# A gated graph network with graph attention on one core: the row of scores through DRAM, pieces made in other ticks, and a new prologue

## The chip, the cores and the metric

The kernel runs on one core of a Trainium2 chip. The metric is device time in microseconds (us) of one launch; the kernel before takes 2248.21 us (median of three runs, 2247.11 to 2249.96). Five engines run side by side, each through its own list of instructions in order: TensorE (PE in the profile, with PEld for its weight loads), VectorE (DVE), ScalarE (ACT), GpSimd (POOL) and SyncE (SP), which here only issues DMA transfers. TensorE multiplies and transposes; its results land in PSUM[...].

## The reference, cut to what matters

There are 64 graphs of 256 nodes with 256 features. Layer 0 is three rounds of a gated graph network with a residual and a layer norm, layer 1 is graph attention with the same.

```python
def _L0_gnn_ref(x, adj, weight, w_ih, w_hh, b_ih, b_hh):
    A = (adj != 0).astype(x.dtype)
    h = x
    for i in range(3):
        m = jnp.einsum('bnd,de->bne', h, weight[i])
        aggr = jnp.einsum('bst,bsd->btd', A, m)
        h = _gru_cell(aggr, h, w_ih, w_hh, b_ih, b_hh)   # r, z, n: sigmoid, sigmoid, tanh
    return h

def _L1_gnn_ref(h, adj, W, a):
    Wh = jnp.matmul(h, W)
    s1 = jnp.einsum('bnf,f->bn', Wh, a[:Fout, 0])
    s2 = jnp.einsum('bnf,f->bn', Wh, a[Fout:, 0])
    e = jax.nn.leaky_relu(s1[:, :, None] + s2[:, None, :], negative_slope=ALPHA)
    attn = jax.nn.softmax(jnp.where(adj > 0, e, NEG_INF), axis=2)
    return jnp.matmul(attn, Wh)

x = _layernorm(x + _L0_gnn_ref(x, adj, ...), axis=-1)
return _layernorm(x + _L1_gnn_ref(x, adj, ...), axis=-1)
```

For each node `n` the attention needs `s2` of every other node side by side in one row, whereas the projection leaves `s2` as a column, one node to a partition. How that column becomes a row is one of the things that change.

## The kernel before

The kernel works on pairs of graphs; there are 32. To keep nearly full precision[...], each operand is cut into pieces: `H` (upper), `L` (lower, source minus `H`) and `D` (a scaled cross term). A gate product is then three matmuls for each 128 x 512 block, two into bank `a` and one into bank `b`, joined by ScalarE and VectorE.

**Ticks.** The program order is made by a small clock. TensorE's gate matmuls are written out in groups of six, and after each group the clock moves by one tick; everything else (aggregation, transposes, attention) is a step that is hung on a tick and is written into its engine's list when the clock reaches it. A block (one round of one pair) has 12 ticks. In the steady state three pairs are under way, so a **turn** has three blocks (rounds 0, 1 and 2 of three pairs) and 36 ticks, and the attention of a fourth pair, with its 72 ticks, lies over two turns.

```python
def product(dst, o, parts, bias=None):
    a, b = bank("pga"), bank("pgb")
    todo = [(a, w[k], m[k], d) for w, m in parts for k in (0, 1) for d in range(C)]     # H, L
    ends = len(todo) - 1
    todo += [(b, w[2], m[2], d) for w, m in parts for d in range(C)]                    # D
    step = len(todo) // len(parts)
    for n, (pt, w, m, d) in enumerate(todo):
        nc.tensor.matmul(pt, w[:, d, o * P:(o + 1) * P], m[:, d, :], ...)               # L369
        if (n + 1) % step == 0 and n + 1 < len(todo):
            tick()
    nc.scalar.activation(dst, a, ..., scale=1.0 + U)                                     # L374, L376
    tick()
    nc.vector.scalar_tensor_tensor(dst, b, -1.0 / U, dst, op0=ALU.mult, op1=ALU.add)    # L378
# ... r, n, z, t for each half e of the features; then tanh, blend (POOL L395, L396), h (DVE L408)
```

A block's input is prepared one block ahead by `front`. `pace` gives the ticks: `turn` (transpose), `split` (`hi`), `rest` (`lo`), `aggregate` (A times hi and lo), `a_upper`, `a_rest`, then the pieces of `h`.

```python
def turn(d):
    s = pairs[p]
    if i == 0:
        src[d] = nodes(s.x, d)
        to_T(s.x, s.hT, d)                                    # L269
    else:
        src[d] = from_T(s.hT, d).rearrange(...)               # L275
def split(d):
    nc.scalar.copy(hi[d], src[d])                             # L306
def rest(d):
    lower(nc.gpsimd if i == 0 else nc.vector, lo[d], src[d], hi[d])      # L132
# ... h_upper (ACT L129), h_lower (POOL L132), h_cross (DVE L135), aggregate (PE L340)
for d in range(C):
    for dt, step in zip(pace[0], (turn, split, rest, aggregate, a_upper, a_rest)):
        at(t + dt + d, lambda step=step, d=d: step(d))
for dt, step in zip(pace[1], (h_upper, h_lower, h_cross)):
    at(t + dt, step)
LOOSE = (2, 3, 4, 6, 7, 8), (5, 8, 10)
```

The attention of a pair, with `t` the tick at which its last block ended (cut; `again`, `halves`, `back`, `join` fetch x and turn the sum back to rows of nodes):

```python
def project(k):
    nc.tensor.matmul(pts[k][:, :D + 2], s.vT[:, d, k * P:(k + 1) * P], gw[:, d, :], ...)  # L493
def spread(k):
    rs = s.rs[:, k:k + 1]
    for dst, src in ((s.s1[:, k:k + 1], pts[k][:, D:D + 1]),
                     (s.s2[:, k, :], pts[k][:, D + 1:D + 2].to_broadcast([P, P])),
                     (s.wh[:, k // C, k % C, :], pts[k][:, :D])): ...     # ACT L502, DVE L504
def rows():
    pts[0] = bank("s2")
    for k in range(K):
        nc.tensor.transpose(pts[0][:, k * P:(k + 1) * P], s.s2[:, k, :], ident)           # L512
def scores():                                                                             # L516
    nc.scalar.activation(s.sc[:, k, :], pts[0][...], AF.Prelu, bias=s.s1[:, k:k + 1], alpha=ALPHA)
def masked():
    nc.vector.copy_predicated(flat(s.sc), flat(s.mask), neg.to_broadcast([P, K * N]))     # L525
# reduce (max, L527), exps (L530), weights_T (L540), combine (L548), add (L554), layer norm, store
```

In the main loop, `begin` (L283, the ones of `adj`) is hung on tick 1 of the front of a new pair, the loads of the next `x` on 7, `masking` (L289) on 19 and the next `adj` on 20. Ahead of the loop a prologue loads and cuts the weights.

Of the kernel before, what the change touches and what calls it, by code (L numbers as in the profile page):

```python
# [26 lines left out]
def kernel(  # L27
# [89 lines left out]
    def flat(t):  # L117
        return t.rearrange("p a b -> p (a b)")
# [63 lines left out]

    wh_n = load_rows(w_hh, ("hH", "hL"), nc.sync)
    wi_n = load_rows(w_ih, ("aH", "aL"), nc.scalar)
# [7 lines left out]
    load_x(0)  # L192
    load_adj(0)
    make_identity(nc, ident)
    nc.gpsimd.memset(half, -0.5)
    nc.gpsimd.memset(neg, NEG_INF)
# [11 lines left out]
    def rows_T(src, use):  # L208
        for c in range(C):
            for o0, o1, t in src:  # L210
                pt = bank("pw")
                for o in range(o1 - o0):
                    nc.tensor.transpose(pt[:, o * P:(o + 1) * P], t[:, o, c * P:(c + 1) * P], ident)
                use(c, o0 * P, o1 * P, pt[:, :(o1 - o0) * P])

    def square_T(src, name):
        pt = bank("pw")
        for e in range(C):
            for d in range(C):
                nc.tensor.transpose(pt[:, (e * C + d) * P:(e * C + d + 1) * P],  # L220
                                    src[:, d, e * P:(e + 1) * P], ident)
        dst = work.tile([P, K, P], F32, tag="hi1", name=name, bufs=1)
        nc.scalar.copy(flat(dst), pt)
        return dst.rearrange("p k n -> p (k n)").rearrange("p (e d) -> p e d", e=C)

    def fold(i, wT, d):
        for o0, o1 in ((0, 512), (512, O)):
            pt = bank("pw")
            for e in range(C):
                nc.tensor.matmul(pt[:, :o1 - o0], wT[:, e, d * P:(d + 1) * P], wih(e, o0, o1),  # L230
                                 start=(e == 0), stop=(e == C - 1))
            cut_weight([t[:, d, o0:o1] for t in wc[i]], pt[:, :o1 - o0], f"{i}_{d}_{o0}")
# [45 lines left out]
    def begin(p):  # L278

        s = pairs[p] = Pair()  # L280
        s.x, s.adj = loaded.pop(p), loaded_adj.pop(p)
        s.A = work.tile([P, G, C, N], F32R, tag="A", name=f"A_{p}", bufs=3)
        nc.vector.tensor_scalar(s.A, s.adj, 0.0, None, op0=ALU.not_equal)  # L283
        s.hT = work.tile([P, C, GN], F32, tag="hT", name=f"hT_{p}", bufs=4)
# [6 lines left out]
    def front(p, i, t, pace):  # L291
# [4 lines left out]
        def turn(d):  # L296
            s = pairs[p]
            if i == 0:
                src[d] = nodes(s.x, d)
                to_T(s.x, s.hT, d)  # L300
            else:
                src[d] = from_T(s.hT, d).rearrange("p (k n) -> p k n", k=K)

        def split(d):
            hi[d] = work.tile([P, K, P], F32R, tag=f"hi{d}", name=f"hi{d}_{nm}", bufs=1)
            nc.scalar.copy(hi[d], src[d])  # L306

        def rest(d):
            lo[d] = work.tile([P, K, P], F32R, tag=f"lo{d}", name=f"lo{d}_{nm}", bufs=1)
            lower(nc.gpsimd if i == 0 else nc.vector, lo[d], src[d], hi[d])  # L310
# [5 lines left out]
        if i == 0:  # L316
            at(t + pace[0][1] + 2, stash)
# [124 lines left out]
    def attention(p, t):  # L442
# [7 lines left out]
        at(t + 5, again)  # L450
# [29 lines left out]
        for d in range(C):  # L480
            at(t + 22 + d, lambda d=d: halves(d))
            at(t + 23 + d, lambda d=d: back(d))
        for g in range(G):
            at(t + 29 + g, lambda g=g: join(g))
        at(t + 30, lambda: setattr(s, "rs", layer_norm(s.v, f"a_{p}", (t + 31, t + 33, t + 34, t + 49))))

        def project(k):
            if k == 0:
                s.s1 = work.tile([P, K], F32, tag="s1", name=f"s1_{p}")
                s.s2 = s.sc[:, :, :P]  # L490
            pts[k] = bank("pwh")
            for d in range(C):
                nc.tensor.matmul(pts[k][:, :D + 2], s.vT[:, d, k * P:(k + 1) * P], gw[:, d, :],  # L493
                                 start=(d == 0), stop=(d == C - 1))

        def spread(k):
            rs = s.rs[:, k:k + 1]
            for dst, src in ((s.s1[:, k:k + 1], pts[k][:, D:D + 1]),
                             (s.s2[:, k, :], pts[k][:, D + 1:D + 2].to_broadcast([P, P])),
                             (s.wh[:, k // C, k % C, :], pts[k][:, :D])):  # L500
                if k < 2:
                    nc.scalar.activation(dst, src, AF.Copy, scale=rs)  # L502
                else:
                    nc.vector.tensor_scalar(dst, src, rs, None, op0=ALU.mult)  # L504
        for k in range(K):
            at(t + 35 + k, lambda k=k: project(k))
            at(t + 36 + k, lambda k=k: spread(k))

        def rows():
            pts[0] = bank("s2")  # L510
            for k in range(K):
                nc.tensor.transpose(pts[0][:, k * P:(k + 1) * P], s.s2[:, k, :], ident)  # L512

        def scores():
            for k in range(K):
                nc.scalar.activation(s.sc[:, k, :], pts[0][:, (k // C) * N:(k // C + 1) * N], AF.Prelu,  # L516
                                     bias=s.s1[:, k:k + 1], alpha=ALPHA)
        at(t + 40, rows)
        at(t + 41, scores)

# [5 lines left out]
        at(t + 42, masked)  # L526
        at(t + 43, lambda: nc.vector.tensor_reduce(s.nm, s.sc, AX.X, ALU.max, negate=True))  # L527
# [4 lines left out]
        for k in range(K):  # L532
            at(t + 47 + k // 2, lambda k=k: exps(k))
        at(t + 52, lambda: nc.vector.reciprocal(s.sm, s.sm))
# [21 lines left out]
        for g in range(G):  # L556
            at(t + 53 + g, lambda g=g: weights_T(g))
            at(t + 54 + g, lambda g=g: nc.vector.tensor_copy(flat(s.sc[:, g * C:(g + 1) * C, :]), pts[g]))
            at(t + 57 + g, lambda g=g: combine(g))
            at(t + 58 + g, lambda g=g: add(g))  # L560
# [4 lines left out]
        at(t + 60, lambda: layer_norm(s.v, f"b_{p}", (t + 61, t + 64, t + 66, t + 70), store))  # L565
# [3 lines left out]
    LOOSE = (2, 3, 4, 6, 7, 8), (5, 8, 10)  # L569

# [4 lines left out]


    rows_T(wh_n, lambda c, o0, o1, pt: cut_weight([t[:, c, o0:o1] for t in whh], pt, f"h{c}_{o0}"))
    begin(0)
    masking(0)
    load_adj(1)  # L580
    rows_T(wi_n, lambda c, o0, o1, pt: evacuate(wih(c, o0, o1), pt))
    nc.vector.tensor_add(b_sum, bi, bh)
    wT = square_T(w_n[0], "wT_0")
    front(0, 0, clock[0], LOOSE)
    for d in range(C):
        fold(0, wT, d)
        tick(3)
# [13 lines left out]
    for n, (p, i) in enumerate(blocks):  # L601
        if n + 1 < len(blocks):
            np_, ni = blocks[n + 1]
            if ni == 0:
                after(1, lambda p=np_: begin(p))
            front(np_, ni, clock[0], CLOSE if n and np_ == blocks[n - 1][0] else LOOSE)
            if ni == 0:
                after(7, lambda p=np_: load_x(p + 1))
                after(19, lambda p=np_: masking(p))
                after(20, lambda p=np_: load_adj(p + 1))  # L610
# [35 lines left out]
```

## Time and profile before

| what | value |
|---|---|
| time, median of three | 2248.21 us |
| span of the profiled execution | 2247.1 us |
| TensorE busy | 2189.0 us (97%) |
| VectorE, ScalarE, GpSimd busy | 1728.2, 1556.4, 1535.2 us |
| one turn in the steady state | 67.4 us, 30 of them with all three blocks |
| mean granted TensorE clock | 0.990 |
| HBM traffic | 39 GB/s over the span |

A turn is the distance between equal instructions of two neighbouring pairs: the transposes of `back`, for example, are issued at 1011.75 us and again at 1079.20 us. The busy time of TensorE counts matmuls that overlap in its pipeline once, so a matmul's own duration (395 ns for one of 512 columns) is longer than its share of a full stream (234 ns, the distance of the starts). What a piece of TensorE work costs is therefore read from starts, not from durations.

### The profile page before, as it was taken

The numbers are of one execution on the slowest core, as the hardware profiler recorded it, in microseconds if no ns is written. First come the engines' busy times: TensorE is split into PE (matmuls) and PEld (weight loads), VectorE is DVE, ScalarE is ACT, GpSimd is POOL, SyncE is SP. The second block draws the span as 40 slices with busy tenths as digits, with TensorE's granted clock in tenths as the row PEclk, the third lists the DMA queues.
The fourth block names the chain that finished last, engine by engine and source line by source line (L and its number), as shares of the span: only waits on it lengthen the run. The fifth ranks groups of instructions, "written<-read, shape, count | busy, mean of one in ns | idle before, by whom it ended". The sixth has DMA issues, their size and how long they took to land.

```text
span 2247.1 us, 31126 instructions
## 1 busy us (share of the span) xinstructions
PE 2189.0 (97%) x10724; PEld 1813.6 (81%) x10724; DVE 1728.2 (77%) x2920; ACT 1556.4 (69%) x2899; POOL 1535.2 (68%) x1084
## 2 busy tenths in 40 slices
PE   7999999999999999999999999999999999999985
PEld 5788888888888888888888888888888888888864
DVE  4667778878778878778878778878778878778875
ACT  4566777677777677777677777677777677777665
POOL 5777667767667767667767667767667767667751
PEclk9999999999999999999999999999999999999997
DMA  3011111111111211112111111111111111111111
GB/s 113 29 38 38 34 42 57 57 48 38 42 43 57 57 47 38 41 45 57 57 48 38 41 45 57 57 48 38 40 46 57 57 48 38 39 47 38 29 38 47
DMA packets 130237, 105.30 MB, mean 47 GB/s; under 512 B 70368, under 2 KB 121824, under 8 KB 130080
## 3 DMA queue, kind: packets, MB, share of 16 engines
q1 hardware_dynamic: 128288, 101.47, 15.4%
q8 instruction: 86, 1.41, 0.3%
q10 hardware_dynamic: 1616, 1.57, 0.2%
q14 instruction: 71, 0.58, 0.1%
q0 software_dynamic: 176, 0.27, 0.1%
HBM read 52.96 MB, written 33.55 MB: 39 GB/s over the span
## 4 chain that ended last, share of the span: by engine, by line
PE 85%; POOL 10%; ACT 1%; DVE 1%; DMA 1%; issue 1%; POOLq 0%; SPq 0%; ACTq 0%; DVEq 0%
PE pga L369 42%; PE pgb L369 21%; PE pa L340 7%; PE po L548 5%; PE pwh L493 5%; POOL t L396 3%; PE pt L275 3%; POOL lo L132 2%; POOL t L395 2%; PE pt L540 1%; POOL n L405 1%; POOL n L401 1%; PE pt L269 1%; POOL rs_b L423 1%; DMA adj<-in_adj_dram 1%
## 5 line engine op out<-in xcount | busy, mean ns | idle before, releaser
L395 POOL TENSOR_TENSOR t<-hT,n 128x512 f32<-128x512 f32 x192 | 288.4, 1502 | 540.1 <-ACT n L387 540.0
L369 PE MATMUL pga<-hH,whhH_whh 128*128 128x512 f32 x1152 | 388.8, 418 | 0.0
L369 PE MATMUL pgb<-hD,whhD_whh 128*128 128x512 f32 x1152 | 362.0, 395 | 0.8 <-DVE hD L135 0.8
L369 PE MATMUL pga<-hL,whhL_whh 128*128 128x512 f32 x1152 | 362.3, 395 | 0.0
L405 POOL TENSOR_TENSOR n<-n,t 128x512 f32<-128x512 f32 x192 | 283.8, 1478 | 57.8 <-DVE t L378 45.5
L396 POOL TENSOR_TENSOR t<-t,z 128x512 f32<-128x512 f32 x192 | 280.6, 1461 | 15.1
L374 ACT ACTIVATE r<-pga 128x512 f32<-128x512 f32 x192 | 114.5, 596 | 235.6 <-PE pga L369 193.0
L369 PEld LDWEIGHTS pgb<-hD,whhD_whh 128*128 128x128 f32 x1152 | 216.3, 188 | 53.3 <-DVE hD L135 1.3
L369 PEld LDWEIGHTS pga<-hL,whhL_whh 128*128 128x128 f32 x1152 | 216.3, 188 | 51.6 <-POOL hL L132 0.2
L401 POOL TENSOR_TENSOR n<-n,r 128x512 f32<-128x512 f32 x192 | 252.8, 1317 | 0.8 <-DVE n L378 0.7
L132 POOL TENSOR_TENSOR hL<-hT,hH 128x1024 fp32r<-128x1024 f32 x96 | 243.8, 2540 | 8.9 <-ACT hH L129 8.9
L376 ACT ACTIVATE n<-pga,bh 128x512 f32<-128x512 f32 x192 | 131.6, 685 | 154.3 <-PE pga L369 154.0
L378 DVE SCALAR_TENSOR_TENSOR r<-pgb,r 128x512 f32<-128x512 f32 x192 | 131.7, 686 | 135.1 <-ACT r L374 75.2
L369 PEld LDWEIGHTS pga<-hH,whhH_whh 128*128 128x128 f32 x1152 | 196.0, 189 | 24.1
L340 PE MATMUL pa<-A,lo 128*128 128x256 f32 x768 | 195.9, 287 | 12.5 <-POOL lo L132 12.4
L340 PE MATMUL pa<-A,hi 128*128 128x256 f32 x768 | 196.5, 287 | 0.0
L378 DVE SCALAR_TENSOR_TENSOR n<-pgb,n 128x512 f32<-128x512 f32 x192 | 131.5, 685 | 67.5 <-ACT n L376 64.5
L387 ACT ACTIVATE z<-z,b_sum 128x512 f32<-128x512 f32 x192 | 141.6, 738 | 43.1 <-DVE z L378 42.7
L340 PEld LDWEIGHTS pa<-A,lo 128*128 128x128 f32 x768 | 146.9, 191 | 27.2 <-POOL lo L132 21.6
L378 DVE SCALAR_TENSOR_TENSOR t<-pgb,t 128x512 f32<-128x512 f32 x192 | 131.7, 686 | 38.5 <-ACT t L374 36.4
L135 DVE SCALAR_TENSOR_TENSOR hD<-hH,hT 128x1024 fp32r<-128x1024 f32 x96 | 156.5, 1630 | 0.0
L340 PEld LDWEIGHTS pa<-A,hi 128*128 128x128 f32 x768 | 146.8, 191 | 7.2
(136 smaller groups left out, 5495.6 us busy)
## 6 DMA issues: line engine op xcount, KB each, us to landing
x<-in_x_dram SPq DMA_DIRECT2D x32, 512.0 KB, 3.9
adj<-in_adj_dram SPq DMA_DIRECT2D x32, 512.0 KB, 3.9
xT<-hT SPq DMA_DIRECT2D x32, 512.0 KB, 2.6
vT<-xT SPq DMA_DIRECT2D x32, 512.0 KB, 3.3
out_dram<-v SPq DMA_DIRECT2D x32, 512.0 KB, 2.9
sc<-wh SPq DMA_TRANSPOSE x64, 3.1
w_n<-in_L_gnn_weight_dram ACTq DMA_DIRECT2D x3, 256.0 KB, 10.3
rows_aH<-in_L_gnn_w_ih_dram ACTq DMA_DIRECT2D x1, 512.0 KB, 6.1
```

Source lines behind the costliest of these rows:

```text
L132: eng.tensor_sub(dst, src, hi.bitcast(F32))
L135: nc.vector.scalar_tensor_tensor(dst, hi.bitcast(F32), 1.0 + U, src, op0=ALU.mult, op1=ALU.subtract)
L340: nc.tensor.matmul(pt[:, g * N:(g + 1) * N], h[:, g * C + c, :], s.A[:, g, c, :], start=(n == 0), stop=(n == len(todo) - 1))
L369: nc.tensor.matmul(pt, w[:, d, o * P:(o + 1) * P], m[:, d, :], start=n in (0, ends + 1), stop=n in (ends, len(todo) - 1))
L374: nc.scalar.activation(dst, a, AF.Copy, scale=1.0 + U)
L376: nc.scalar.activation(dst, a, AF.Identity, scale=1.0 + U, bias=bias)
L378: nc.vector.scalar_tensor_tensor(dst, b, -1.0 / U, dst, op0=ALU.mult, op1=ALU.add)
L387: nc.scalar.activation(dst, dst, func, bias=bias)
L395: nc.gpsimd.tensor_sub(t, h, n)
L396: nc.gpsimd.tensor_mul(t, t, z)
L401: after(2, lambda r=r, n=n: nc.gpsimd.tensor_mul(n, n, r))
L405: after(1, lambda n=n, t=t: nc.gpsimd.tensor_add(n, n, t))
```

## The change

It does five things.

1. **Row of s2 through DRAM.** `spread` writes `s1` and `s2` of a block as two neighbouring values. The column of `s2` is written to DRAM by one small DMA and read back by a second one, broadcast to all partitions. The four transposes, their bank and the two broadcast copies on ScalarE and two on VectorE go. ScalarE makes the scores from SBUF, in two steps.
2. **Pieces of x in other ticks.** For round 0 a third pace, FIRST, makes `hi` and `lo` of x two ticks earlier.
3. **Another timetable of the attention.** The layer norm, projection, combination and store come two to four ticks earlier; scores, masking and maximum come three ticks later than before.
4. **Mask and load of adj** move from ticks 19 and 20 to 22 and 23.
5. **Prologue in another order.** x is loaded and turned first, the ScalarE table for the sigmoid is loaded at once, the weights come in parts.

```diff
+    load_x(0)
     wh_n = load_rows(w_hh, ("hH", "hL"), nc.sync)
+    load_adj(0)
     wi_n = load_rows(w_ih, ("aH", "aL"), nc.scalar)
...
-    load_x(0)
-    load_adj(0)
...
+    nc.scalar.activation(warm, half, AF.Sigmoid)
...
         def rest(d):
-            lower(nc.gpsimd if i == 0 else nc.vector, lo[d], src[d], hi[d])
+            lower(nc.gpsimd if i == 0 and p else nc.vector, lo[d], src[d], hi[d])
...
-        at(t + 5, again)
+        at(t + 9, again)
...
-            at(t + 22 + d, lambda d=d: halves(d))
-            at(t + 23 + d, lambda d=d: back(d))
+            at(t + 21 + d, lambda d=d: halves(d))
+            at(t + 22 + d, lambda d=d: back(d))
         for g in range(G):
-            at(t + 29 + g, lambda g=g: join(g))
-        at(t + 30, lambda: setattr(s, "rs", layer_norm(s.v, f"a_{p}", (t + 31, t + 33, t + 34, t + 49))))
+            at(t + 26 + g, lambda g=g: join(g))
+        at(t + 27, lambda: setattr(s, "rs", layer_norm(s.v, f"a_{p}", (t + 28, t + 30, t + 31, t + 35))))
...
-            at(t + 35 + k, lambda k=k: project(k))
-            at(t + 36 + k, lambda k=k: spread(k))
+            at(t + 32 + k, lambda k=k: project(k))
+            at(t + 33 + k, lambda k=k: spread(k))

         def rows():
-            pts[0] = bank("s2")
-            for k in range(K):
-                nc.tensor.transpose(pts[0][:, k * P:(k + 1) * P], s.s2[:, k, :], ident)
+            s.row = far.tile([P, K], F32, tag="row", name=f"row_{p}", bufs=2)
+            nc.sync.dma_start(s.row, s.s12[:, 1, :])
+        def rows_back():
+            s.s2 = s.vT[:, 0, :]
+            nc.sync.dma_start(s.s2, s.row.rearrange("n k -> (n k)").partition_broadcast(P))
...
-        at(t + 40, rows)
-        at(t + 41, scores)
+        at(t + 37, rows)
+        at(t + 38, rows_back)
+        for g in range(G):
+            at(t + 43 + g, lambda g=g: scores(g))
...
-        at(t + 42, masked)
-        at(t + 43, lambda: nc.vector.tensor_reduce(s.nm, s.sc, AX.X, ALU.max, negate=True))
+        at(t + 45, masked)
+        at(t + 46, lambda: nc.vector.tensor_reduce(s.nm, s.sc, AX.X, ALU.max, negate=True))
...
-            at(t + 47 + k // 2, lambda k=k: exps(k))
-        at(t + 52, lambda: nc.vector.reciprocal(s.sm, s.sm))
+            at(t + 48 + k // 2, lambda k=k: exps(k))
+        at(t + 50, lambda: nc.vector.reciprocal(s.sm, s.sm))
...
-            at(t + 53 + g, lambda g=g: weights_T(g))
-            at(t + 57 + g, lambda g=g: combine(g))
+            at(t + 52 + g, lambda g=g: weights_T(g))
+            at(t + 55 + g, lambda g=g: combine(g))
...
+    FIRST = (2, 1, 2, 6, 7, 8), (5, 8, 10)
...
+    front(0, 0, clock[0] + 1, ((0, 1, 2, 9, 11, 12), (7, 8, 13)))
...
-                after(19, lambda p=np_: masking(p))
-                after(20, lambda p=np_: load_adj(p + 1))
+                after(22, lambda p=np_: masking(p))
+                after(23, lambda p=np_: load_adj(p + 1))
```

## The prediction

> **What bounds the kernel now.** I read the page's busy rows and chain first, then a table of stages (one turn of the steady state alone), then TensorE's waits in that stretch, and last the timelines of single engines, because in a kernel with a timetable only the order inside one turn tells what a moved step will meet.
>
> ```profile
> PE 2189.0 (97%) x10724; PEld 1813.6 (81%) x10724; DVE 1728.2 (77%) x2920; ACT 1556.4 (69%) x2899; POOL 1535.2 (68%) x1084
> PE 85%; POOL 10%; ACT 1%; DVE 1%; DMA 1%; issue 1%; POOLq 0%; SPq 0%; ACTq 0%; DVEq 0%
> ```
>
> TensorE is busy 97% of the span and carries 85% of the chain that ended last. The next view gives one turn (start:end and length, then busy time of PE, PEld, DVE, ACT, POOL, clock, DMA share, GB/s), and under it the whole list of TensorE's waits between 270 and 2090 us:
>
> ```profile
> 1012.00:1079.40 67.40, 67.10 (x333) 55.82 (x333) 53.24 (x91) 48.24 (x91) 47.37 (x33) 1.00 0.17 48
> PE pa L340 <- POOL lo L132: 8.1, 27, 0.3
> ```
>
> So in a turn of 67.40 us TensorE stands still for 0.30 us, always at the same place: the aggregation waits for `lo`, which GpSimd makes. The next busiest engine, VectorE, works 53.24 us of it. From the starts in TensorE's timeline the turn can be added up: 216 gate matmuls at 0.2335 us = 50.4; 48 of the aggregation at 0.119 = 5.7; 4 projections at 0.87 = 3.5; 2 combinations at 1.71 = 3.4; 9 groups of four transposes at 0.44 = 3.9; together 66.9, and about 0.56 for the wait. That gives 67.5, so nothing else is hidden in it. The kernel is bound by TensorE's own work. Only three things can move the time: TensorE work taken out, waits removed or created in the turn (each counts 30 times), and the two ends.
>
> [...] the spacing of the starts, not the 97%, is what I build on. [...] the 512 KB write of `xT` lands after 2.6 us, the read of `vT` after 3.3. No small DMA of this kind runs before the change[...]. [...] `hD`, the same instruction each time, takes 1.22 us or 2.32 us.
>
> **1. The transposes that go.** Their place in the turn:
>
> ```profile
> 1043.31 0.63 PE L369 MATMUL pga<-aH,wc0H_wc 128*128 128x512 f32 x2
> 1043.78 0.60 PE L512 MATMUL s<-ident,sc 128*128 128x128 f32 x4
> 1044.13 0.71 PE L369 MATMUL pga<-aL,wc0L_wc 128*128 128x512 f32 x2
> 1044.68 0.63 PE L369 MATMUL pgb<-hD,whhD_whh 128*128 128x512 f32 x2
> ```
>
> The four take 0.35 us to the next start, and the two matmuls behind them 0.55 instead of 0.47: 0.35 + 0.08, 0.44 us with rounding. Gain 0.44 us a turn. Two ScalarE copies of 364 ns and two VectorE copies of 342 ns also go; both engines are off the path.
>
> **2. The wait for lo.**
>
> ```profile
> 1025.31 0.28 PE L340 MATMUL pa<-A,hi 128*128 128x256 f32 x1
> 1025.89 0.39 PE L340 MATMUL pa<-A,lo 128*128 128x256 f32 x1 [0.30 <-POOL lo L132]
> 1026.11 0.28 PE L340 MATMUL pa<-A,hi 128*128 128x256 f32 x1
> ```
>
> From the first of these to the third there are 0.80 us; undisturbed it would be two steps of 0.12. The wait thus costs 0.56 us, of which only 0.30 is marked as idle. The cause is order: GpSimd makes this `lo` at 1024.54, behind the two steps of a blend (1021.66 and 1023.23). FIRST puts both `lo` at ticks 26 and 27, ahead of the blend at tick 29. GpSimd should then have the second some 2 us before TensorE wants it. Gain 0.56 us a turn.
>
> **3. The later masking.** Here I expect a loss. The page is no help; VectorE's list in ticks 6 to 10 is:
>
> ```profile
> 1046.97 1.40 DVE L525 COPY_PREDICATED_SCALAR sc<-mask,neg 128x1024 f32 x1 [0.40 <-ACT sc L516]
> 1049.01 1.21 DVE L527 TENSOR_REDUCE nm<-sc 128x4 f32<-128x1024 f32 x1
> 1050.14 0.95 DVE L289 TENSOR_SCALAR mask<-adj 128x1024 uint8<-128x1024 int32 x1
> 1052.20 0.68 DVE L378 SCALAR_TENSOR_TENSOR r<-pgb,r 128x512 f32<-128x512 f32 x1
> 1055.20 2.32 DVE L135 SCALAR_TENSOR_TENSOR hD<-hH,hT 128x1024 fp32r<-128x1024 f32 x1
> ```
>
> and TensorE's needs are (tick 8, and the first use of that `hD` in tick 13):
>
> ```profile
> 1051.69 0.63 PE L369 MATMUL pga<-hH,whhH_whh 128*128 128x512 f32 x2
> 1059.16 0.63 PE L369 MATMUL pgb<-hD,whhD_whh 128*128 128x512 f32 x2
> ```
>
> Now `hD` ends at 1057.52, 1.64 us before use. The three long VectorE steps lie in ticks 6 and 7, ahead of the result of `r`. After the change masking is at tick 9 (45), the maximum at 10 (46), `masking` at 10 (24 + 22 - 36), and all three enter the list ahead of `h_cross`, the step that makes `hD`, since they were hung up earlier. By starts they are 1.43 + 1.13 + 0.87 = 3.43 us. VectorE can't start them sooner, because `r` needs TensorE's tick 8. From tick 8 to the use TensorE has 7.47 us of work before and after. VectorE begins `r` 0.25 us sooner, with no backlog, so `hD` comes 3.2 us later in relation to TensorE if it stays slow, 2.1 if it runs in 1.22. Against 1.64 of slack that is a wait of 0.45 to 1.55 us. GpSimd's blend of tick 11 ends about where `hD` starts, so I choose a mostly fast one: loss 0.8 us a turn.
>
> **4. The DMA round trip and the other ticks.** `s2` leaves at tick 37, scores are made at 43; six ticks with TensorE's inserted work are some 10 us[...]. Hidden in the steady state. Projections move in front of the turn's border at equal cost. `join` now has 4 ticks after the transposing DMAs (3.1 us to landing) instead of 6, some 3 us to spare by my count. The second `hD` (tick 22) keeps about 1 us. I count nothing for these.
>
> **5. The ends.** In the prologue TensorE's waits were 6.4 us for the first weights, 4.3 for `lo` (GpSimd still cutting weights) and 0.8 for `hD`; the first `pgb` matmul ran at 32.80 us. With x first, `lo` on VectorE and the weights in parts, VectorE sets the pace: cuts of whh 4.4, `lo` 1.4, cuts of wc0 4.4, A and mask 1.4, a_rest 2.6, hD 1.2, evacuations 1.5, 17 us in all from about 8 or 9 us. First `pgb` at about 26: gain 7 us. The tail of some 65 us after the last gates has nothing to hide a round trip behind[...]; loss 4 us.
>
> **Sum.** 30 turns x (-0.44 - 0.56 + 0.8) = -6; prologue -7; tail +4. 2248.2 - 9 = 2239 us.
>
> **Rivals.** (a) The VectorE order does no harm: then a turn gains 1.0 us, 30 in all, and the time is about 2215. For it speaks VectorE's idle time of 14 us a turn; against it that none of it lies between ticks 8 and 10. (b) The masking chain costs more: a slow `hD`, or scores late because of the round trip, 1.6 us a turn or more; then 2263 and above. Exponentials at tick 12 are two ticks behind the maximum instead of four, so ScalarE's banks could hold TensorE too. (c) Only the ends and the transposes matter, with `lo` replaced by an equal wait elsewhere: 2248 - 13 - 3, about 2232.
>
> **Range and chances.** The terms of the turn are uncertain by about 0.5 us, 15 us in all, the ends by 5. Predicted 2239 us, 2215 to 2261 eight times in ten. Over 2% faster (below 2203) needs all gains and no new wait, and still lacks 10 us: 0.05. Over 2% slower (above 2293) needs 1.8 us more of waits a turn than I see: 0.04. Within 2%: 0.91.
>
> **What would show it.** TensorE's waits in the steady stretch: `pa <- POOL lo` gone; `pgb <- DVE hD` about 30 times, some 0.8 us each. Turn 67.2 us. No wait of ScalarE's scores for a DMA until the tail. First `pgb` near 26 us. The prediction is wrong if the turn has another wait than hD (banks, join, `r`), or none.

## The result, and the profile after

The changed kernel takes 2324.4 us (median of four runs, 2321.78 to 2326.74); beside it the kernel before takes 2247.66 us. The ratio is 1.034, with a 95% interval of 1.0322 to 1.0358: 77 us slower, where 9 us faster had been predicted, and outside the range of 2215 to 2261.

The page of the kernel after, its row of busy times and its chain by engine:

```profile
PE 2178.4 (94%) x10596; PEld 1812.0 (78%) x10596; DVE 1732.0 (75%) x2858; ACT 1569.1 (68%) x2835; POOL 1484.2 (64%) x1082
PE 55%; POOL 19%; DVE 11%; ACT 7%; issue 6%; DMA 1%; POOLq 0%; ACTq 0%; SPq 0%; DVEq 0%
```

TensorE has 128 matmuls less (10724 before) and is busy for 10.6 us less, in a span that is 75 us longer: 94% instead of 97%. Its share of the chain falls from 85% to 55%. What it lost went to waits, and those stand in the list of TensorE's waits from 300 to 2090 us (total, times, longest):

```profile
PE pgb L376 <- DVE hD L135: 61.8, 26, 2.4
PE pga L376 <- DVE aD L135: 12.3, 25, 0.5
```

The wait for `lo` is gone, as predicted. The wait for `hD` is there about once per turn, as predicted, but with 2.4 us instead of 0.8. The wait for `aD` was not predicted. The third finding is in the turns. The times of the transfer that brings x back for `join` (the same instruction of each pair) are 67.44 us apart in every turn of the kernel before. Now they are 69.07 or 70.65 us apart, in almost regular alternation, 69.77 in the mean. Two neighbouring turns (start:end, length, busy PE, PEld, DVE, ACT, POOL, granted clock, DMA share, GB/s):

```profile
1003.25:1073.91 70.66, 67.78 (x330) 56.53 (x329) 53.53 (x88) 48.84 (x89) 45.61 (x33) 0.98 0.18 49
1073.91:1142.99 69.08, 66.22 (x330) 55.32 (x329) 53.43 (x88) 48.65 (x89) 45.56 (x33) 1.00 0.18 50
```

The same 330 matmuls keep TensorE busy for 1.56 us more in the longer turn, and only there the clock is below 1.00. So a turn holds two losses: a wait, and in nearly half of the turns slower matmuls behind it.

VectorE's list in ticks 8 to 11 of the kernel after, the stretch that step 3 of the prediction was about (start, duration, instruction, idle time before it in brackets):

```profile
1072.90 0.69 DVE L385 SCALAR_TENSOR_TENSOR r<-pgb,r 128x512 f32<-128x512 f32 x1 [1.50 <-PE pgb L376]
1073.92 1.39 DVE L536 COPY_PREDICATED_SCALAR sc<-mask,neg 128x1024 f32 x1 [0.32 <-ACT sc L525]
...
1076.97 1.22 DVE L538 TENSOR_REDUCE nm<-sc 128x4 f32<-128x1024 f32 x1
1078.10 1.37 DVE L295 TENSOR_SCALAR mask<-adj 128x1024 uint8<-128x1024 int32 x1
1079.39 1.76 DVE L415 TENSOR_TENSOR hT<-t,n 128x512 f32<-128x512 f32 x1
1081.07 1.21 DVE L135 SCALAR_TENSOR_TENSOR hD<-hH,hT 128x1024 fp32r<-128x1024 f32 x1
```

The order is the predicted one: masked, maximum, mask, then the addition of h, then `hD`. From `r` to the end of `hD` it takes 9.38 us, where the prediction's list came to 7.65. TensorE wanted `hD` at 1079.9; it came at 1082.3. TensorE in the same turn, and in the one before it:

```profile
1011.77 0.70 PE L376 MATMUL pgb<-hD,whhD_whh 128*128 128x512 f32 x2 [2.38 <-DVE hD L135]
...
1014.44 1.05 PE L376 MATMUL pga<-hL,whhL_whh 128*128 128x512 f32 x2
1015.29 1.05 PE L376 MATMUL pgb<-hD,whhD_whh 128*128 128x512 f32 x2
...
1079.43 0.61 PE L376 MATMUL pga<-aL,wc1L_wc 128*128 128x512 f32 x2
1082.43 0.70 PE L376 MATMUL pgb<-hD,whhD_whh 128*128 128x512 f32 x2 [2.38 <-DVE hD L135]
...
1084.34 0.62 PE L376 MATMUL pga<-hL,whhL_whh 128*128 128x512 f32 x2
1084.80 0.62 PE L376 MATMUL pgb<-hD,whhD_whh 128*128 128x512 f32 x2
```

From 1079.43 to 1082.43 there are 3.00 us where 0.46 would do: the wait costs 2.54 us. In the first of the two turns the pairs of matmuls behind it last 1.05 instead of 0.62 us. Two stretches of each turn, each 3.41 us long, which is how long the clock stays low, show why (behind the length stands TensorE's busy time; the granted clock is the last column but two):

```profile
1009.37:1012.79 3.42, 1.04 (x6) 0.83 (x6) 3.42 (x4) 2.18 (x3) 0.57 (x1) 1.00 0.57 158
1012.79:1016.20 3.41, 3.41 (x12) 2.73 (x11) 1.34 (x3) 3.38 (x10) 1.28 (x1) 0.50 0.00 0
1077.64:1081.06 3.42, 2.41 (x11) 1.67 (x9) 3.42 (x3) 0.00 (x0) 2.96 (x2) 1.00 0.13 12
1081.06:1084.47 3.41, 2.04 (x11) 1.76 (x12) 2.42 (x4) 3.20 (x7) 0.85 (x1) 1.00 0.43 144
```

The clock is halved from 1012.79 to 1016.20, that is after TensorE has started again, and then is full. These 3.41 us at half speed are the 1.57 us by which the turns differ.

Why only some turns are hit can be worked out from the trace. All changes of the clock in it lie whole multiples of 3.413 us apart: the falls at 384.74, 524.68, 664.63 and 872.84 us, for example, are 41, 41 and 61 such steps apart, and each lasts one step. In the step before each of the 11 falls between 300 and 2090 us TensorE stood still for 1.93 us or more; in every other step it stood still for 1.86 us or less. The first turn's wait lies inside one step, with 2.38 us of standing still; the second's is cut by a border into 1.01 and 1.37. Two turns (139.72 us) are nearly 41 steps (139.95), and so hits and misses nearly alternate.

The granted clock has two values in this trace, 1.00 and 0.50, and between 300 and 2090 us some 1.9 us of standing still within one step of 3.41 us are enough for the lower one.

### The profile page after: what moved, and what is told of

It reads as the page before. It is cut to its first block, busy times and chain, and to the rows that moved or that the text cites. A ratio compares the mean times of both kernels' runs of the same rounds, so it can differ in the third digit from the quotient of the medians.

```text
span 2322.2 us, 30795 instructions
## 1 busy us (share of the span) xinstructions
PE 2178.4 (94%) x10596; PEld 1812.0 (78%) x10596; DVE 1732.0 (75%) x2858; ACT 1569.1 (68%) x2835; POOL 1484.2 (64%) x1082
## 3 DMA queue, kind: packets, MB, share of 16 engines
q10 hardware_dynamic: 1616, 1.57, 0.2%
## 4 chain that ended last, share of the span: by engine, by line
PE 55%; POOL 19%; DVE 11%; ACT 7%; issue 6%; DMA 1%; POOLq 0%; ACTq 0%; SPq 0%; DVEq 0%
PE pga L376 26%; PE pgb L376 12%; PE pa L347 6%; PE po L559 5%; POOL t L402 4%; POOL lo L132 3%; POOL t L403 3%; POOL n L408 3%; PE pt L279 3%; PE pwh L499 2%; DVE hT L415 2%; POOL n L412 2%; ACT sc L525 2%; DVE aD L135 2%; DVE nm L538 2%
## 5 line engine op out<-in xcount | busy, mean ns | idle before, releaser
L402 POOL TENSOR_TENSOR t<-hT,n 128x512 f32<-128x512 f32 x192 | 290.1, 1511 | 610.9 <-ACT n L394 610.8
L376 PE MATMUL pga<-hH,whhH_whh 128*128 128x512 f32 x1152 | 395.8, 425 | 13.2 <-DVE aD L135 13.2
L412 POOL TENSOR_TENSOR n<-n,t 128x512 f32<-128x512 f32 x192 | 260.6, 1357 | 105.7 <-DVE t L385 95.7
L408 POOL TENSOR_TENSOR n<-n,r 128x512 f32<-128x512 f32 x192 | 264.1, 1375 | 3.9 <-DVE n L385 3.8
L403 POOL TENSOR_TENSOR t<-t,z 128x512 f32<-128x512 f32 x192 | 253.1, 1318 | 15.0
L381 ACT ACTIVATE t<-pga 128x512 f32<-128x512 f32 x192 | 114.8, 598 | 195.9 <-DVE hT L415 131.2
L132 POOL TENSOR_TENSOR hL<-hT,hH 128x1024 fp32r<-128x1024 f32 x96 | 230.2, 2397 | 10.6 <-ACT hH L129 10.5
L415 DVE TENSOR_TENSOR hT<-t,n 128x512 f32<-128x512 f32 x192 | 193.3, 1007 | 6.7 <-POOL t L403 6.7
L132 DVE TENSOR_TENSOR aL<-pa,aH 128x512 fp32r<-128x512 f32 x192 | 130.7, 681 | 38.7 <-ACT aH L129 38.7
```

The lines of the kernel that those rows point to most:

```text
L132: eng.tensor_sub(dst, src, hi.bitcast(F32))
L381: nc.scalar.activation(dst, a, AF.Copy, scale=1.0 + U)
L402: nc.gpsimd.tensor_sub(t, h, n)
L403: nc.gpsimd.tensor_mul(t, t, z)
L408: after(2, lambda r=r, n=n: nc.gpsimd.tensor_mul(n, n, r))
L412: after(1, lambda n=n, t=t: nc.gpsimd.tensor_add(n, n, t))
```

## The experiments

The rivals when the experiments began: **O**, the order on VectorE (the later maximum, masking and mask stand ahead of `h_cross`), and **R**, the round trip of the row through DRAM, with its late scores. All runs in one table; "turn" is the mean distance in the steady state.

| kernel | what it is | time, us | ratio to before, 95% interval | turn, us |
|---|---|---|---|---|
| before | | 2247 | 1 | 67.44 |
| after | | 2324.4 | 1.0322 to 1.0358 | 69.77 |
| e1_behind | after, maximum and mask behind h_cross | 2291.3 | 1.0183 to 1.0214 | 68.63 |
| e2_early | after, scores, masking, maximum, mask three ticks earlier | 2251.2 | 1.0008 to 1.0023 | 67.29 |
| e3_transposes | after, with transposes for the row | 2318.2 | 1.0301 to 1.0332 | 69.67 |
| e4_late | before, with masking, maximum, mask at the new ticks | 2351.5 | 1.0448 to 1.048 | 71.11 |
| e5_tail | e2_early, transposes in the last three pairs | 2248.2 | 0.9998 to 1.0015 | 67.32 |
| e6_shift | e5_tail, the layer norm's shift three ticks later | 2228.8 | 0.9902 to 0.9935 | 66.56 |
| e7_mask | e6_shift, mask behind h_cross | 2207.7 | 0.9807 to 0.9836 | 65.83 |
| e8_filler | after, ten useless matmuls in the wait | 2300.3 | 1.0224 to 1.0255 | 69.07 |
| e9_loose | e7_mask, pieces of x at the old ticks | 2232.9 | 0.9918 to 0.9951 | 66.74 |
| e10_alltr | e7_mask, transposes in all pairs | 2215.9 | 0.9845 to 0.9875 | 66.15 |
| e11_maskonly | after, mask alone behind h_cross | 2282.4 | 1.0141 to 1.0172 | 68.44 |
| e12_prologue | before, new prologue alone | 2227.2 | 0.9889 to 0.9922 | 66.89 |
| e13_shift32 | before, tiles 32 bytes further | 2229.2 | 0.9899 to 0.9935 | 66.89 |
| e14_shift64 | e7_mask, tiles 32 bytes further | 2224.1 | 0.9873 to 0.9909 | 66.39 |

### e1_behind: maximum and mask behind h_cross

```diff
-        at(t + 46, lambda: nc.vector.tensor_reduce(s.nm, s.sc, AX.X, ALU.max, negate=True))
+        at(t + 47, lambda: nc.vector.tensor_reduce(s.nm, s.sc, AX.X, ALU.max, negate=True))
-                after(22, lambda p=np_: masking(p))
-                after(23, lambda p=np_: load_adj(p + 1))
+                after(23, lambda p=np_: masking(p))
+                after(24, lambda p=np_: load_adj(p + 1))
```

> The changed kernel, with only the maximum and the mask of the next pair moved one tick back, so that both stand behind h_cross in VectorE's list (masking itself stays in front). Theory O (order: what costs is the VectorE work that now stands ahead of hD): the maximum and the mask are 1.1 and 1.3 us of the wait of 2.4, so the wait falls to 0 to 0.3 us, a turn to about 67 us, and the time to 2235 to 2260. Rival R (row: the round trip through DRAM and the slower reading of the scores are what costs): the row is untouched, so 2310 to 2325.

2291.3 us, 33 us less than after, but not in the expected range. TensorE's waits from 300 to 2050 us:

```profile
PE pgb L376 <- ACT r L381: 33.4, 26, 1.3
PE pga L376 <- DVE aD L135: 11.9, 25, 0.5
PE pgb L376 <- DVE hD L135: 10.7, 26, 0.4
```

The wait for `hD` falls to 0.4 us, so what stands ahead of `h_cross` does decide it. But a new wait takes its place: the exponentials, first in ScalarE's list, now stand for the later maximum, and the evacuation of `r` behind them frees TensorE's bank late. Moving a piece back by a tick only moved the wait.

### e2_early: the old ticks, with the row through DRAM

```diff
-            at(t + 43 + g, lambda g=g: scores(g))
+            at(t + 40 + g, lambda g=g: scores(g))
-        at(t + 45, masked)
-        at(t + 46, lambda: nc.vector.tensor_reduce(s.nm, s.sc, AX.X, ALU.max, negate=True))
+        at(t + 42, masked)
+        at(t + 43, lambda: nc.vector.tensor_reduce(s.nm, s.sc, AX.X, ALU.max, negate=True))
-                after(22, lambda p=np_: masking(p))
-                after(23, lambda p=np_: load_adj(p + 1))
+                after(19, lambda p=np_: masking(p))
+                after(20, lambda p=np_: load_adj(p + 1))
```

> The changed kernel, with scores, masking, maximum, mask and load of adj three ticks sooner, at the ticks of the kernel before; the row still goes through DRAM. In the trace of the changed kernel the row lands about 2 us before ScalarE would come to the scores then. Theory O: no wait for hD, a turn of 66.5 us, 2220 to 2245. Rival R: the round trip doesn't fit into the shorter time, ScalarE waits for the DMA in every turn and TensorE behind it: 2290 or more.

2251.2 us: 73 of the 77 us are back with three ticks, and the row still goes through DRAM. (Masking, maximum and mask stand at their old ticks here, two of the four scores one tick ahead of theirs.) No instruction of ScalarE waits for the row in the steady state. The round trip of R falls: the transfers fit into three ticks fewer than they were given. Left are a wait of 0.6 us for `hD`, the one of 0.5 for `aD`, and a long tail. The cause of the `aD` wait can be read in VectorE's list of this kernel:

```profile
1084.66 1.25 DVE L433 SCALAR_TENSOR_TENSOR nmr_a<-mv_a,rs_a 128x4 f32<-128x4 f32 x1 [1.20 <-POOL rs_a L430]
```

This is the `shift` of the attention's layer norm. It is a step of 0.15 us, but VectorE stands in it for 1.2 us until GpSimd has `rs_a`, and the pieces of the aggregation stand behind it.

### e3_transposes: the late ticks, with the old transposes

```diff
-            nc.sync.dma_start(s.row, s.s12[:, 1, :])
+            for k in range(K):
+                nc.tensor.transpose(pts[0][:, k * P:(k + 1) * P], s.s2[:, k, :], ident)
... (s.s2 by broadcast copies, scores from PSUM, as in the kernel before)
```

> The changed kernel, with the four transposes and the copies of before in place of the row through DRAM; scores stay at ticks 43 and 44 and everything else as changed. Theory O: the wait for hD stays, somewhat shorter (about 2.0 us) because scores from PSUM take 0.48 us where those from the row take 0.75; 0.44 us of transposes come back: 2300 to 2325. Rival R: the loss goes with the row: 2235 to 2260.

2318.2 us, as O has it. Without any row through DRAM nearly all of the loss stays. TensorE's wait from 300 to 2090 us, and its transposes in one turn:

```profile
PE pgb L376 <- DVE hD L135: 49.0, 26, 1.9
1064.61 0.60 PE L519 MATMUL s<-ident,sc 128*128 128x128 f32 x4
1064.96 0.72 PE L376 MATMUL pga<-aL,wc0L_wc 128*128 128x512 f32 x2
1065.51 0.62 PE L376 MATMUL pgb<-hD,whhD_whh 128*128 128x512 f32 x2
```

The transposes take 0.35 us and the matmuls behind them 0.55 instead of 0.46: 0.44 us a turn. The wait for `hD` is 0.49 us shorter, 1.89 instead of 2.38, because ScalarE reads the scores from PSUM and masked starts 0.61 us behind `r` instead of 1.02. The two cancel. So 1.9 us of the wait stay without the row, as O has it, and R holds for 0.5: not by the transfers, for which nothing waits in e2_early, but by the late scores. The mean granted clock of e3_transposes is 0.980, against 0.976 in the changed kernel and 0.987 in e2_early.

### e4_late: the late ticks in the kernel before

```diff
-        at(t + 42, masked)
-        at(t + 43, lambda: nc.vector.tensor_reduce(s.nm, s.sc, AX.X, ALU.max, negate=True))
+        at(t + 45, masked)
+        at(t + 46, lambda: nc.vector.tensor_reduce(s.nm, s.sc, AX.X, ALU.max, negate=True))
-            at(t + 47 + k // 2, lambda k=k: exps(k))
+            at(t + 48 + k // 2, lambda k=k: exps(k))
-                after(19, lambda p=np_: masking(p))
-                after(20, lambda p=np_: load_adj(p + 1))
+                after(22, lambda p=np_: masking(p))
+                after(23, lambda p=np_: load_adj(p + 1))
```

> The kernel before, with only masking, maximum, mask and load of adj moved to the ticks of the change (exponentials one tick later to stay behind the maximum). Theory O: this alone makes TensorE wait for hD in each of 30 turns, 1.5 to 2.4 us: 2290 to 2325. Rival R: nothing about the row is changed: 2243 to 2258.

2351.5 us, 104 more than before and more than either theory expected. The direction is O's. The wait for `hD` is 1.7 us here, and a second one of 0.7 us, for a `lo` of VectorE, comes with it; the granted clock is 0.991 in the mean, against 0.976 in the changed kernel, and between 1000 and 1400 us no pair of gate matmuls lasts more than 0.82 us. The turn is 3.67 us longer. By starts, against the same instructions of the kernel before, the wait for `hD` costs 1.93 of them and that for `lo` 0.94; 0.77 are lost in small pieces at the transposes of the attention's weights between the two. Why these come late was not followed.

### e5_tail: is the tail the row?

```diff
+            if p >= NP - 3:
+                todo.append((s.s2[:, k, :], pts[k][:, D + 1:D + 2].to_broadcast([P, P])))
... (transposes and scores from PSUM for these pairs only)
```

> The kernel of e2_early (the changed kernel with scores, masking and maximum three ticks earlier), in which the last three pairs make their rows with transposes again, so that no DMA stands in the chain after the last gate product; the steady turns stay as they are. If the tail of 80 us (66 in the kernel before) is due to the round trips of the row in series, as the chain of e2_early suggests: 13 us less than its 2251, about 2238, with some 67 us from the last gate products to the end. If the tail is longer for another reason (the other timetable of the attention, the layer norm at the end), the time stays within 4 us of 2251.

Only 3 us less. From the last gate product to the end the kernel before takes 66.0 us, after 79.9, e2_early 80.0, e5_tail 75.2. So the row is worth 4.8 us of the tail. Its transfers stand in the chain of e2_early one behind another (start, length):

```profile
2203.26 3.75 DMA vT<-row
...
2213.22 3.52 DMA row<-s
2216.79 3.34 DMA vT<-row
```

The other 9 us remain when they are gone. By elimination they lie in the new timetable of what is left at the end; which step it is wasn't tried. The later masking and maximum are not it: e4_late, which has them in the kernel before, has a tail of 63.3 us.

### e6_shift and e7_mask: the two waits that are left

```diff
-  layer_norm(s.v, f"a_{p}", (t + 28, t + 30, t + 31, t + 35))      # e5_tail
+  layer_norm(s.v, f"a_{p}", (t + 28, t + 30, t + 34, t + 35))      # e6_shift
-                after(19, lambda p=np_: masking(p))                # e6_shift
-                after(20, lambda p=np_: load_adj(p + 1))
+                after(23, lambda p=np_: masking(p))                # e7_mask
+                after(24, lambda p=np_: load_adj(p + 1))
```

> e5_tail with one more number changed: the shift of the attention's layer norm stands three ticks later in VectorE's list, where GpSimd's result for it should be there. If the 0.5 us per turn that TensorE waits for aD comes from VectorE standing in that shift, the wait goes and with it 0.5 to 0.66 us in 30 turns: 15 to 20 us, from about 2238 to about 2220. If the wait for aD has another cause (GpSimd slowing VectorE's adds), the time stays within 5 us of e5_tail and the aD wait stays at 0.4 to 0.5.

> e6_shift with the making of the next pair's mask moved four ticks later (19 to 23, and the load of adj with it), so that it stands behind h_cross in VectorE's list instead of ahead of it. If the rest of the wait for hD (0.6 us per turn in e2_early) is the order on VectorE, the mask's 1.3 us no longer stands ahead of h_cross, the wait goes, and the time falls by about 0.6 in 30 turns, 18 us, to about 2203. If the rest of the wait is VectorE and GpSimd slowing each other while h_cross adds, the wait stays above 0.4 and the time within 6 us of e6_shift.

e6_shift: 19 us less; the wait for `aD` is gone and the turn 0.76 us shorter. e7_mask: another 21 us, and no wait is left in the list of TensorE's waits. One turn of e7_mask:

```profile
1010.00:1075.84 65.84, 65.84 (x330) 55.40 (x329) 54.64 (x90) 48.74 (x89) 46.95 (x34) 1.00 0.19 53
```

TensorE is busy for all of the 65.84 us. At 2207.65 us this version beats both kernels: 1.8% below the one before (0.9807 to 0.9836), with FIRST, the new prologue, and the row through DRAM in all pairs but the last three.

### e8_filler: why the clock falls

```diff
+        def filler():
+            pt = bank("fill")
+            for n in range(10):
+                nc.tensor.matmul(pt, whh[0][:, 0, :P], whh[0][:, 0, :512], start=(n == 0), stop=(n == 9))
+        at(t + 49, filler)
```

> The changed kernel with ten matmuls of 512 columns, whose result nobody reads, put on TensorE where it stands for hD (2.4 us per turn): TensorE is then busy for most of that wait, and hD comes no earlier. If the fall of the granted clock in about half of the turns[...] comes of TensorE having stood still, it no longer falls, all turns take about 69.1 us, and the time goes from 2324 to about 2300. If the clock falls for the load of the turn or of the chip, it falls with the filler as often or oftener, and the time stays at 2324 or rises by up to 0.3 us per turn, to 2333.

2300.3 us: ten matmuls that do nothing useful make the kernel 24 us faster. All 26 turns now take 69.0 to 69.1 us. The 8 us from the start of the filler:

```profile
1069.40:1077.40 8.00, 7.88 (x40) 6.21 (x39) 5.40 (x7) 6.08 (x13) 2.50 (x2) 1.00 0.21 66
```

TensorE is busy for 7.88 of 8 us and the clock is 1.00. The fall of the clock (to 0.50 for 3.41 us in the changed kernel) came of standing still.

### e9_loose and e10_alltr: what the two gains are worth

```diff
-  LOOSE if ni else FIRST)         # e7_mask
+  LOOSE)                          # e9_loose
```

e10_alltr has the branch of e5_tail for every pair.

> The kernel of e7_mask with one part of the change undone: the new pieces of x (FIRST) are made at the old ticks again. Theory: the old pace makes TensorE wait for lo once per turn, 0.56 us in the kernel before, so 30 turns take 17 us more: about 2224, with the wait of pa for lo back at 0.4 to 0.7 us per turn. Rival: with VectorE relieved in those ticks the pieces come in time also at the old pace, and the time stays within 6 us of 2207.

> The kernel of e7_mask with another part undone: all pairs make their rows with transposes and ScalarE reads them from PSUM, and no row goes through DRAM. Theory: the four transposes take 0.44 us per turn on TensorE, which has no idle time left in e7_mask, so the time is 13 us more: about 2220. Rival: the strided reads of the row by ScalarE (747 against 481 ns each, four per turn) and the two transfers cost as much as the transposes save, and the time stays within 5 us of 2207 or falls.

e9_loose: 25 us more, the turn 0.90 us longer, and the old wait is back:

```profile
PE pa L347 <- POOL lo L132: 16.8, 26, 0.7
```

e10_alltr: 8 us more, the turn 0.32 us longer. So the row through DRAM does save time. By starts the transposes cost 0.45 us a turn here, as counted in the prediction. Part of it comes back: in e7_mask the first two matmuls with `hD` lose 0.15 us, too little to be listed as a wait, and in e10_alltr, where the scores come sooner, they lose nothing.

### e11_maskonly: one number, one tick

```diff
-                after(22, lambda p=np_: masking(p))
-                after(23, lambda p=np_: load_adj(p + 1))
+                after(23, lambda p=np_: masking(p))
+                after(24, lambda p=np_: load_adj(p + 1))
```

> The changed kernel with a single number moved by one tick: the making of the next pair's mask at 23 instead of 22 (and the load of adj at 24), so that it stands behind h_cross in VectorE's list; the maximum stays ahead of it. Theory of the order on VectorE: hD comes earlier by the mask's 1.3 us, the wait for it falls from 2.4 to about 1.1 us, and a wait so short no longer lets the granted clock fall: the turn goes from 69.8 to some 67.7 us and the time from 2324 to about 2262 (2250 to 2275). Rival: h_cross waits for GpSimd's blend and not for the mask; then the wait stays at 2 us or more and the time above 2305.

2282.4 us: 42 us less for one number, where 62 were expected. The wait fell from 2.4 to 1.8 us, not to 1.1. VectorE's list of this kernel:

```profile
1059.37 1.21 DVE L538 TENSOR_REDUCE nm<-sc 128x4 f32<-128x1024 f32 x1
1060.49 1.36 DVE L415 TENSOR_TENSOR hT<-t,n 128x512 f32<-128x512 f32 x1
1061.77 2.30 DVE L135 SCALAR_TENSOR_TENSOR hD<-hH,hT 128x1024 fp32r<-128x1024 f32 x1
1064.00 0.68 DVE L295 TENSOR_SCALAR mask<-adj 128x1024 uint8<-128x1024 int32 x1
```

The mask no longer stands ahead, and takes 0.68 instead of 1.37 us. But `hD` now lies beside a step of GpSimd (L408, from 1061.27 for 1.72 us) and takes 2.30 us instead of 1.21: the slowing fell on the instruction that was there. By starts: 1.29 for the mask and 0.40 for the addition won, 1.09 for `hD` lost, 0.60 net, which is the 0.6 by which the wait fell. All turns are equal again (68.40 to 68.47 us) and the granted clock is 0.989 in the mean, against 0.976: the wait of 1.8 us leaves the clock alone here. Per turn 0.6 for the wait and 0.70 for the clock make 1.30 of the 1.33 us measured.

### e12_prologue, e13_shift32, e14_shift64: a gain that nobody meant

```diff
     neg = const.tile([P, 1], F32, name="neg")
+    shim = const.tile([P, K], F32, name="shim")     # e13_shift32: before; e14_shift64: e7_mask
+    nc.gpsimd.memset(shim, 0.0)
```

> The kernel before with the new prologue alone (x first, weights in parts, the warm tile, lo of the first pair on VectorE); its turn, its pace and its attention stay. If the new prologue is worth what the first gate product for hD showed (27.1 instead of 32.8 us): 6 us less than before, about 2241, with turns of 67.44 us as before. There is one thing more to be told apart: in all kernels made from the changed one, gate matmuls in parts of the turn start 0.227 us apart instead of 0.233, some 0.6 us per turn. If that comes with the prologue (tiles lie elsewhere in SBUF because of the new order), the turn falls to about 66.8 us and the time to 2222. If it comes with the other timetable, the turn stays at 67.44.

> The kernel before with one unused tile of 32 bytes per partition declared ahead of the work tiles (one memset of it on GpSimd, no other instruction changed): all tiles that TensorE streams lie 32 bytes further, on multiples of 64 bytes instead of 32 beside them. If the faster stream of gate matmuls in the kernels with the new prologue comes of where the tiles lie: the turn falls from 67.44 to about 66.9 and the time by 16 us, to about 2231. If it comes of the order of the prologue or of the early load of ScalarE's table: the turn stays at 67.44 and the time within 3 us of 2247.

> The kernel of e7_mask with the same unused tile: its streamed tiles, on multiples of 64 bytes so far, lie 32 bytes beside them again. If the place of the tiles decides: gate matmuls start 0.233 us apart throughout, the turn goes from 65.84 to about 66.4 and the time from 2207 to about 2224. If it doesn't: the time stays within 3 us of 2207.

The new prologue alone makes the kernel before 20 us faster, and shortens every turn by 0.55 us, although it changes no instruction of a turn. An unused tile, which takes up 32 bytes per partition, does the same: 19 us, the same turn of 66.89 us. In e7_mask the same tile does the opposite, by 0.56 us per turn and 16 us. TensorE's stream at one place of the kernel before:

```profile
1014.16 0.63 PE L369 MATMUL pga<-hL,whhL_whh 128*128 128x512 f32 x2
1014.63 0.63 PE L369 MATMUL pga<-aH,wc2H_wc 128*128 128x512 f32 x2
1015.10 0.63 PE L369 MATMUL pga<-aL,wc2L_wc 128*128 128x512 f32 x2
1015.57 0.63 PE L369 MATMUL pgb<-hD,whhD_whh 128*128 128x512 f32 x2
```

and at the same place of e13_shift32:

```profile
1004.03 0.61 PE L371 MATMUL pga<-hL,whhL_whh 128*128 128x512 f32 x2
1004.48 0.62 PE L371 MATMUL pga<-aH,wc2H_wc 128*128 128x512 f32 x2
1004.94 0.62 PE L371 MATMUL pga<-aL,wc2L_wc 128*128 128x512 f32 x2
1005.39 0.61 PE L371 MATMUL pgb<-hD,whhD_whh 128*128 128x512 f32 x2
```

The starts are 0.47 us apart for two matmuls above and 0.453 below. In the kernel before the tiles that TensorE streams begin 32 bytes past a multiple of 64 (as built, x lies at byte 93024 of each partition); the prologue's small `warm` tile moves them to a multiple of 64 (93056), and so does the unused tile. In e14_shift64 they are 32 bytes past one again (93088), and the starts 0.467 us apart again. That the place decides is shown in both directions, by these two places alone; but all tiles declared behind the unused one move together, so which of them matters stays open, and so does why the place matters, and why only in parts of the turn.

The prologue's own worth is what e12_prologue has beyond e13_shift32: 2 us, within the uncertainty of the two.

## Why the prediction was wrong, step by step

**Step 1, transposes gone, 0.44 us a turn.** Right, in size too: by starts the transposes cost 0.44 us (e3_transposes) and 0.45 (e10_alltr). But the slower reading of the row takes some of it back: 0.32 us are left in e7_mask, and nothing in the changed kernel, where the reading lengthens the wait for `hD` by 0.49.

**Step 2, the wait for lo gone, 0.56 us.** Right in cause; worth 0.90 us against e7_mask.

**Step 3, the later masking: the step that failed.** The mechanism was right: three VectorE instructions ahead of `h_cross`, a wait for `hD` once per turn, and `hD` itself fast (1.21 us), as chosen. The size was not: 2.54 us instead of 0.8. With a fast `hD` the working gave 0.45 us of wait; the list took 1.73 us more than its sum, together some 2.2, and the trace marks 2.4. Three terms carry it. Masked began 0.42 us later than right behind `r`, because the scores came late: ScalarE takes 747 ns for each, reading the row from SBUF at every fourth value, instead of 481 from PSUM, a difference that I left out (e3_transposes, which undoes it, waits 0.49 us less). The mask took 1.29 us by starts instead of 0.87. And the addition of h took 1.68 instead of 0.60: the prediction took its durations from a list in which GpSimd's blend fell on `hD` (2.32 us), and by letting `hD` run fast it let this slowing vanish. It only moved to the instructions ahead: between 300 and 2000 us the 97 additions of h that take 0.68 us have no GpSimd step beside them, and the 49 slow ones (1.67 us in the mean) all have one. (Not each GpSimd step slows each instruction: 48 of the 73 `hD` in that stretch have one beside them, L402, and take 1.21 us.) The three terms are 1.92 us; masked itself, 1.26 by starts instead of 1.43, gives 0.17 back. Rival (b), "1.6 us a turn or more; then 2263 and above", came true in size, but not as it was argued: `hD` was not slow, and its "scores late" are 0.42 of the 1.92 us and come from the reading of the row, not from the round trip.

**A term that was missing: the clock.** 2.4 us of standing still halve the clock behind it in nearly every second turn: 1.57 us there, 0.70 in the mean (69.77 against 69.07 in e8_filler).

**Step 4, round trip hidden, other ticks nothing.** The first half is right (e2_early). The transfers take 1.6 and 3.8 us (medians), 5.4 together, inside the six ticks that the prediction put at some 10. The second half is wrong: the layer norm's shift at its new tick costs 0.76 us a turn (e6_shift).

**A gain that was missing: the place of the tiles**, 0.55 us a turn.

The turn adds up, each term from the run that isolates it: 67.44, minus 0.55 for the place, 0.90 for lo and 0.32 for the transposes, is 65.67 (e7_mask: 65.83). Plus 0.73 and 1.75 for what stands ahead of `h_cross` (e7_mask to e6_shift, e5_tail to e8_filler), 0.76 for the shift and 0.70 for the clock, from e7_mask's 65.83: 69.77, the turn of the kernel after. The terms depend on the order in which they are taken out; the sum closes by construction, except for the 0.16 us between 65.67 and 65.83.

**Step 5, the ends.** The first `pgb` matmul with `hD` starts at 27.09 us instead of 32.80: 5.7 us of the predicted 7. But most of the lead is lost again in the first turns. In e12_prologue TensorE waits 2.3 us for the attention's weights (`gwT`) between 60 and 80 us (0.9 in e13_shift32), and the granted clock of these 20 us is 0.91 in the mean, which is what 3.41 us at half speed make, against 1.00 in e13_shift32. The transfer that brings the first pair's x back is issued at 154.35 us, against 155.53 in e13_shift32: 1.2 us are left. The tail is 14 us longer instead of 4: the row itself was sized well (4.8; the 4 was an estimate of mine that no trace of before shows, as no small transfer of this kind ran there), the 9 us of the other timetable were not seen.

By spans: the last gate product comes 61 us later and the tail is 14 us longer, 75 together. Thirty turns of 2.33 us would make 70; the 9 us that lack are the shorter start and, by difference only, the blocks at both ends that gain from the place of the tiles without having the waits.

## What to carry to other kernels

In a kernel with a timetable, follow the instruction that moves through the list of its engine down to the next thing that the bound engine waits for, and give the instructions ahead of it the durations that fit their new neighbours: here the slowing beside GpSimd did not go away, it landed on what stood there (the addition of h, 1.67 us instead of 0.68; in e11_maskonly `hD`, 2.30 instead of 1.21). Ask also how fast the consumer reads the new place of its data (here 747 ns instead of 481). A wait on the bound engine can cost more than its length: here the clock fell behind waits of 2.4 us in nearly every second turn, 1.57 us each time. A cheap filler tells whether that happens. And before a gain is put down to a new order, undo the addresses: an unused tile of 32 bytes per partition moved this kernel by 19 us, twice what its whole change was predicted to bring.

## What the runs showed of the hardware that I had not expected

- In the traces of the kernels before and after TensorE's granted clock changes on a grid of 3.413 us, between 1.00 and 0.50. From 300 to 2090 us of the kernel after it is 0.50 for one step behind each step in which TensorE stood still for 1.93 us or more (11 of them), and 1.00 behind each with 1.86 us or less. That is no threshold for the whole program: it also fell behind a step with 1.81 us at 64 us, and in the kernel before behind one with 1.00 us at 70 us. Waits of 2.4 us are hit in nearly every second turn; with waits of 1.8 us (e11_maskonly) all turns are equal, and with 1.7 us (e4_late) the mean clock is 0.991.
- Gate matmuls of 512 columns start 0.227 us apart in parts of a turn in e13_shift32, where the streamed tiles begin at a multiple of 64 bytes, and 0.233 us apart at the same place of the kernel before, where they begin 32 bytes beside it: 0.55 us of a turn of 67 us. Only these two places were run.
- ScalarE takes 747 ns for 256 values at every fourth place of an SBUF row, and 481 ns for 256 neighbouring ones in PSUM. No run here separates the step from the change of memory.
- A small write of a column to DRAM (2 KB) is read back, broadcast to all partitions, within 5.4 us (medians 1.6 and 3.8) to 6.9 us (3.5 and 3.3, in the tail), both transfers together, and beside TensorE's work no engine waited for it (e2_early).
